# A planned kernel of four graph layers: LSTM gates by Tanh alone, the planner's order held on four engines, its margins drawn from a list

## The chip, the cores and the metric

The kernel runs on one core of one Trainium2 chip. The metric is the time of one execution on the device in microseconds (us); less is better. Times before and after are medians of several runs. A profile comes from one execution, taken by the hardware profiler.

In a core, TensorE (PE) multiplies matrices from SBUF into PSUM, and its weight loads (PEld) have a row of their own. VectorE (DVE), ScalarE (ACT) and GpSimd (POOL) work on elements, and SyncE (SP) issues DMAs. Each engine takes its instructions from a queue of its own, in a fixed order, and waits on semaphores for the others.

## What is computed

The input x has 128 graphs of 64 nodes with 256 features, in float32; all graphs share one 64x64 adjacency. Four layers follow, each closed by a residual sum and a LayerNorm:

```python
x = _layernorm(x + _L0_gnn_ref(x, adj, ...))   # normalised aggregation, two dense layers, two batch norms
x = _layernorm(x + _L1_gnn_ref(x, adj, ...))   # Laplacian (by its largest eigenvalue), attention, Gelu MLP
x = _layernorm(x + _L2_gnn_ref(x, adj, ...))   # two GCN layers, then LSTMs over windows of 1, 2, 3 and 4 nodes
x = _layernorm(x + _L3_gnn_ref(x, adj, ...))   # graph attention
```

The LSTM of layer 2 is the part whose formulas the change rewrites. Its last state overwrites the last node of each window, and the next window length reads what the one before wrote:

```python
g = x_t @ Wih.T + h @ Whh.T + bias
i, f, gg, o = jnp.split(g, 4, axis=-1)
c = sigmoid(f) * c + sigmoid(i) * tanh(gg)
h = sigmoid(o) * tanh(c)
```

## The kernel before, in words

The 8192 rows are cut into 16 blocks of 512 rows. A block is held in SBUF either with rows on the partitions (4 tiles of 128x256) or with features on the partitions (2 tiles of 128x512). Working memory is planned by hand: four PSUM tiles of 128x1024 (`PS`), and a stock of SBUF slots of the same size (`mem`) that grows as constants and earlier results fall out of use.

The order of the work is planned in Python while the program is written. Each task is a generator (`first_block`, `second_block`, `end_block`, `block`, `gcn_block`, `unit`, `last_block`, and a few for weights). At each `yield step(engine, us, ...)` (line 121) it says which engine its next instructions use, how long the planner should take them to last, how many PSUM tiles and slots they take, and from when they can run. `flow` (line 130) holds a clock for each engine. Again and again it picks one waiting step, advances the clock, and lets the generator write that step's instructions. Line 177 is the rule of choice: a step's time is the larger of its engine's free time and its own ready time plus the engine's margin. The earliest time wins, and ties go to the stream with the lower priority number. A margin so lets a step of a better stream pass another that would be ready a little earlier. Margins are 2.0 us for TensorE and 0.5 for VectorE and ScalarE (line 30). A step that names an activation table costs 1.3 us more when the table differs from the last one named (line 190).

There are two flows. The first (line 700) runs the eigenvalue loop and layer 0 up to its second batch norm. The second (line 1677) runs the rest in parallel streams: the blocks of layer 1 with the end of layer 0 (`seq`), the GCN with the one-step LSTM (`gcn`), the LSTM units of 2, 3 and 4 steps (`units`), and layer 3 (`last`, and `end` for the last four blocks in halves). The last three units have a stream of their own that needs no margin.

What the planner writes is not what the engines get. The framework's scheduler orders each engine's instructions again by its own estimate before it sets the waits.

The lines that the change touches:
- `stats` (line 264): bn_stats (L272) and bn_aggr (L273) for each of a block's four rows of tiles, then L274. Its users raise the result to the power -0.5 on POOL (L282, L294, L308).
- `ln_affine_steps` (line 289): LayerNorm with gain and bias on VectorE, two instructions per tile (L297, L300). `block` uses it twice.
- `ln_steps_act` (line 302): LayerNorm without them; VectorE makes -mean/std (L311), ScalarE applies it, one instruction per tile (L314).
- `lstm` (line 1036): one unit. The first step has no state: `products` (L1055), `gates` (L1067, bias inside), the product of i and tanh(g) on POOL (L1086), Tanh of the cell (L1094), the product with o on VectorE (L1102, or L1357 and L1389 where it is the last step). Later steps multiply by a Strassen scheme with seven products instead of eight (L1127), with sums on POOL (L1147, L1175) and VectorE (L1171, L1173, L1193, L1195), evictions on VectorE (L1186), gates on ScalarE (L1203, L1205, L1207), the product of i and tanh(g) on POOL (L1220), the cell on VectorE (L1228, L1231) and its Tanh (L1236).
- `plain_steps` (line 1251): later steps of the two half units at the end, without Strassen (L1264, L1266; gates L1269; the product on POOL L1280).
- Other long instructions on POOL: L634 in layer 0; L822, L860, L915, L916 and L933 in layer 1.
- Exp is at L854 and L1544, Gelu at L928. Evictions of PSUM that stand in the prediction: L749, L772, L898, L948, L1325 and L1345 on VectorE, L784 and L1353 on ScalarE.

Of the kernel before, what the change touches and what calls it, by code (L numbers as in the profile page):

```python
# [19 lines left out]
NT = 4  # L20
# [9 lines left out]
MARGIN = {"T": 2.0, "V": 0.5, "S": 0.5}  # L30
# [3 lines left out]
def kernel(ctx: ExitStack, tc: tile.TileContext, a: dict, out: bass.AP):  # L34
    nc = tc.nc
    V, S, G, T = nc.vector, nc.scalar, nc.gpsimd, nc.tensor

# [83 lines left out]
    def step(e, us, ps=0, sl=0, waits=True, at=None, tbl=None):  # L121

        return (e, us, ps, sl, waits, at, tbl)

    def flow(streams, margin):  # L130
# [6 lines left out]
        free = dict.fromkeys("TVSGQ", 0.0)  # L137
        table, running, now, seq = None, [], 0.0, 0
        while True:
# [31 lines left out]
            for r in running:  # L171
                e, us, ps, sl, _, at, tbl = r[2]
                at = at() if callable(at) else at
                if r[2][5] is not None and at is None:
                    continue
                t = r[3] if at is None else at
                soon = max(t if r[6].urgent else t + margin.get(e, 0.0), free[e])
                t = max(t, free[e])
                if (ps <= 0 or len(PS.free) >= ps) and (sl <= 0 or (len(mem.free) >= sl and safe(r, sl))):
                    if ps > 0:  # L180
                        t = max(t, PS.free[0][0])
                        soon = max(soon, PS.free[0][0])
                    if sl > 0:
                        t = max(t, heapq.nsmallest(sl, mem.free)[-1][0])
                        soon = max(soon, t)
                    if best is None or soon < least - 1e-9:
                        best, when, least = r, t, soon
            assert best is not None, "no task can go on"
            e, us, ps, sl, waits, at, tbl = best[2]
            if tbl is not None and tbl != table:  # L190
                us, table = us + 1.3, tbl
            end, now = when + us, when
# [84 lines left out]
    def ln_steps(y):  # L277

        yield step("V", 2.45)
# [3 lines left out]
        yield step("V", 1.9)  # L283
# [5 lines left out]
    def ln_affine_steps(y, g, b):  # L289

        yield step("V", 2.45)
        mv, rs = stats(y)
        yield step("G", 1.0)
        G.tensor_tensor(rs, rs, neghalf[:, :NT], ALU.pow)  # L294
        yield step("V", 3.4)
        for t in range(NT):
            V.scalar_tensor_tensor(y[:, t, :], y[:, t, :], mv[:, t, 0:1], g, ALU.subtract, ALU.mult)  # L297
            o = b if len(b.shape) == 2 else b[:, t, :]
            dst = y if len(b.shape) == 2 else b
            V.scalar_tensor_tensor(dst[:, t, :], y[:, t, :], rs[:, t : t + 1], o, ALU.mult, ALU.add)  # L300

    def ln_steps_act(y):

        n = y.shape[1]
        yield step("V", 0.6 * n)
# [6 lines left out]
        yield step("S", 0.6 * n)  # L312
# [93 lines left out]
    with c0:  # L406
# [129 lines left out]
        def bn_coeffs(name, nch, st, g, be):  # L536
# [4 lines left out]
            yield step("V", 0.3 * nch)  # L541
# [16 lines left out]
        def first_block(i):  # L558
# [6 lines left out]
            yield step("T", 1.15, ps=1, sl=1)  # L565
# [25 lines left out]
        def second_block(i):  # L591
# [27 lines left out]
            yield step("S", 2.8)  # L619
# [6 lines left out]
            yield step("V", 1.4, sl=2)  # L626
# [6 lines left out]
            yield step("G", 1.3, waits=False)  # L633
            G.tensor_tensor(T4, h[:, :, u], T2, ALU.subtract)  # L634
            yield step("V", 0.7)
# [98 lines left out]
    def end_block(i):  # L734
# [4 lines left out]
        yield step("S", 1.4)  # L739
# [15 lines left out]
    def block(i):  # L755
        x = X[i]
        mark("begun", i)
        yield step("T", 1.15, ps=1, sl=1)
# [15 lines left out]
        yield from ln_affine_steps(y, rows[:, names.index("g1"), :], rows[:, names.index("be1"), :])  # L774
        yield step("V", 1.25)
# [25 lines left out]
        yield step("T", 3.6, ps=1, sl=1)  # L801
# [19 lines left out]
        yield step("G", 2.4, waits=False)  # L821
# [3 lines left out]
        yield step("T", 1.15, ps=1, sl=1)  # L825
# [17 lines left out]
        yield step("V", 1.4, ps=-1)  # L843
# [5 lines left out]
        yield step("V", 2.5)  # L849
# [9 lines left out]
        yield step("G", 1.9)  # L859
# [13 lines left out]
        yield step("T", 1.15, ps=1, sl=1)  # L873
# [40 lines left out]
        yield step("G", 4.7, waits=False)  # L914
# [3 lines left out]
        for hf in range(2):  # L918
# [6 lines left out]
            yield step("S", 1.4, ps=-1, waits=hf == 1, tbl="gelu")  # L925
# [6 lines left out]
        yield step("G", 2.4, waits=False)  # L932
# [17 lines left out]
        yield from ln_affine_steps(y, rows[:, names.index("g3"), :], x)  # L950
# [25 lines left out]
    V.tensor_tensor(bl, bl, bh, ALU.add)  # L976

    def gcn_rows():
# [15 lines left out]
        PS.give(ps)  # L994
        mark("rows")
# [29 lines left out]
    def lstm(p, n, parts, x_of, out_of):  # L1025

        us = n * 1.68e-3
        v_us, g_us, s_us = (0.05 + n * r for r in (1.25e-3, 2.3e-3, 1.15e-3))  # L1030

        def bias(g, c):
            return bl[:, p - 1, 2 * g + c : 2 * g + c + 1]
# [30 lines left out]
        def gates(pair, t, ps, sl):  # L1064
            t = yield step("S", 0.1 + n * 2.5e-3, ps=-1, at=t, waits=False, tbl="sigmoid")
            for j, (g, c) in enumerate(pair):
                S.activation(of(sl)[:, j], fm(PS[ps])[:, j, :n], AF.Tanh if g == 2 else AF.Sigmoid, bias=bias(g, c))  # L1067
# [13 lines left out]
        for c in range(2):  # L1081
# [3 lines left out]
            t = yield step("G", g_us, at=t, waits=False)  # L1085
            G.tensor_tensor(of(s_cell)[:, c], of(sl)[:, 0], of(sl)[:, 1], ALU.mult)  # L1086
# [3 lines left out]
        for c in range(2):  # L1090
            sl = (sa, sb)[c]
            th = of(sl)[:, 1]
            t = yield step("S", s_us, at=tc_[c], waits=False, tbl="sigmoid")
            S.activation(th, of(s_cell)[:, c], AF.Tanh)  # L1094
            o = of(s_o)[:, c]
            t = yield step("V", v_us, at=max(t, t_o), sl=0 if p == 1 or c else 1, waits=False)
            if p == 1:
                last_h(c, o, th)
            else:
                if c == 0:  # L1100
                    s_h = mem.take()
                V.tensor_tensor(of(s_h)[:, c], o, th, ALU.mult)  # L1102
# [4 lines left out]
        if len(parts) == 1 and p > 1:  # L1107
            yield from plain_steps(p, n, us, of, bias, x_of, lambda ap: spread(ap, 0), last_h, s_cell, s_h, h_at)
# [27 lines left out]
        for s in range(1, p):  # L1136
# [3 lines left out]
            t_1 = yield step("G", g_us, sl=2, at=0.0, waits=False)  # L1140
# [28 lines left out]
            def differences():  # L1169
                yield step("V", two_us, at=h_at, waits=False)  # L1170
                V.tensor_tensor(T2, h_v, T1, ALU.subtract)  # L1171
                t_h.append((yield step("V", two_us, at=h_at, waits=False)))
                V.tensor_tensor(shaped(T3), shaped(h_v), x_v, ALU.subtract)  # L1173
                t_h.append((yield step("G", g_us, at=t_h[1], waits=False)))
# [22 lines left out]
            def stage4(g):  # L1197
                v, y = places(g)
                f = AF.Tanh if g == 2 else AF.Sigmoid
                t = yield step("T", us, at=max(t_h[2], at[g]), waits=False)  # L1200
                product(g, "A22", T4, v[:, 0, :])
                yield step("S", 0.1 + n * 1.15e-3, at=at[g, "0"], waits=False, tbl="sigmoid")
                S.activation(of(act[g])[:, 0], of(act[g])[:, 0], f, bias=bias(g, 0))  # L1203
                yield step("S", copy_us, at=at[g], waits=False, tbl="sigmoid")
                S.activation(y[:, 3, :], y[:, 3, :], f, bias=bias(g, 1))  # L1205
                at[g] = yield step("S", copy_us, ps=-1, at=t, waits=False, tbl="sigmoid")
                S.activation(y[:, 2, :], v[:, 0, :], f, bias=bias(g, 1))  # L1207
# [11 lines left out]
            t_g = yield step("G", 2 * g_us, at=at[2], waits=False)  # L1219
            G.tensor_tensor(of(act[2]), of(act[0]), of(act[2]), ALU.mult)  # L1220
# [6 lines left out]
            yield step("V", 2 * v_us, at=at[1], waits=False)  # L1227
            V.tensor_tensor(cell, cell, of(act[1]), ALU.mult)  # L1228
            mem.give(act[1])
            t = yield step("V", 2 * v_us, at=t_g, waits=False)  # L1230
            V.tensor_tensor(cell, cell, of(act[2]), ALU.add)  # L1231
# [3 lines left out]
            t = yield step("S", 2 * s_us, at=t, waits=False, tbl="sigmoid")  # L1235
            S.activation(of(act[2]), cell, AF.Tanh)  # L1236
            t = yield step("V", 2 * v_us, at=max(t, at[3]), sl=0 if last else 1, waits=False)
# [3 lines left out]
            else:  # L1241
                s_h = mem.take()
                V.tensor_tensor(of(s_h), of(act[3]), of(act[2]), ALU.mult)
# [6 lines left out]
    def plain_steps(p, n, us, of, bias, x_of, shaped, last_h, s_cell, s_h, h_at):  # L1250

        v_us, g_us, s_us = (0.05 + n * r for r in (1.25e-3, 2.3e-3, 1.15e-3))
        for s in range(1, p):
# [3 lines left out]
            def products(pair):  # L1257
# [9 lines left out]
                t = yield step("S", 0.3 + n * 2.1e-3, ps=-1, at=t, waits=False, tbl="sigmoid")  # L1267
                for j, (g, c) in enumerate(pair):
                    S.activation(of(sl)[:, j], fm(PS[ps])[:, j, :n], AF.Tanh if g == 2 else AF.Sigmoid, bias=bias(g, c))  # L1269
# [4 lines left out]
            for c in range(2):  # L1274
# [4 lines left out]
                tg = yield step("G", g_us, at=ta, waits=False)  # L1279
                G.tensor_tensor(A[:, 1], A[:, 0], A[:, 1], ALU.mult)  # L1280
                t = yield step("V", v_us, at=tb, waits=False)
                V.tensor_tensor(cell, cell, F[:, 0], ALU.mult)
                t = yield step("V", v_us, at=max(t, tg), waits=False)
                V.tensor_tensor(cell, cell, A[:, 1], ALU.add)
                t = yield step("S", s_us, at=t, waits=False, tbl="sigmoid")
                S.activation(A[:, 1], cell, AF.Tanh)
                ends.append((c, t, sa, sb))

            for c, t, sa, sb in ends:
                t = yield step("V", v_us, at=t, sl=0 if last or c else 1, waits=False)  # L1290
                if last:
                    last_h(c, of(sb)[:, 1], of(sa)[:, 1])
                else:
                    if c == 0:
                        h_new = mem.take()
                    V.tensor_tensor(of(h_new)[:, c], of(sb)[:, 1], of(sa)[:, 1], ALU.mult)
# [9 lines left out]
    def gcn_block(i):  # L1306
        yield step("T", 1.15, ps=1, sl=1)
# [21 lines left out]
        yield step("T", 1.15, ps=1, sl=1)  # L1329
# [12 lines left out]
        yield step("V", 1.4, ps=-1)  # L1342
# [13 lines left out]
        def out_of(q, c, o, th):  # L1356
            V.tensor_tensor(  # L1357
                hT_block(i)[:, c, :, :].rearrange("p n b -> p b n"), o, th, ALU.mult
# [9 lines left out]
    def unit(p, g, w0, nw, b0, nb):  # L1368
# [19 lines left out]
        def out_of(q, c, o, th):  # L1388
            V.tensor_tensor(half(src[:, c, :, p - 1, :], q), o, th, ALU.mult)  # L1389
# [22 lines left out]
    def sum_weights(p, sums):  # L1412
# [18 lines left out]
        for k in range(2):  # L1431
            i0, i1, h0, h1 = (w[:, k, :, c, :] for w in (ih, hh) for c in range(2))
            s1, s2, s3, s4 = (gates(sums[2 * i + k]) for i in range(4))
            for dst, y, z, op in (
# [5 lines left out]
                yield step("V", 0.7)  # L1440
# [15 lines left out]
    def last_block(i, t0=0, nt=NT):  # L1456
# [6 lines left out]
        yield step("S", 2.2 * r, sl=1)  # L1463
# [14 lines left out]
        V.tensor_tensor(x, px, x, ALU.add)  # L1478
# [260 lines left out]
```

## Time and profile before

| | |
|---|---|
| median of 3 runs (lowest, highest) | 2408.22 us (2407.28, 2410.26) |
| the profiled execution | 2409.44 us |
| its span, first to last instruction | 2407.7 us |
| mean granted TensorE clock | 0.982 of full speed |
| TensorE busy, idle in the span | 2287.2 us, 120.5 us |
| VectorE, ScalarE, POOL busy | 1287.7, 1187.4, 591.7 us |

The profile's busy time of an engine is the time in which one of its instructions runs. A group's row names line, engine, operation, output and inputs, shape and count; behind the bar are busy time, mean ns of one and the idle time just before them with what ended it. A timeline's row has start, duration, engine and line; in square brackets the idle time before it and the instruction that ended it. A row of the waits reads: who waited, for whom, us in total, times, longest. The granted clock is the share of TensorE's full speed that the hardware allowed. Times within the span are counted from its first instruction.

### The profile page before, as it was taken

To read this page: it belongs to the slowest core of one execution; us is meant where nothing else is said; L and a number is where in the kernel's file an instruction comes from. 1 tells how busy PE (TensorE), PEld (TensorE's weight loads), DVE (VectorE), ACT (ScalarE), POOL (GpSimd) and SP (SyncE) were. 2 spreads that over 40 slices of the span, in tenths; PEclk is the share of its full clock that TensorE was granted. 3 is DMA by queue.
4 is the path that set the end of the run, shared out by engine and by line. 5 is a ranking of instruction groups with operands and counts; after the bars stand their busy time and mean duration, and the time that the engine had idled before them with its cause. 6 is when DMAs were issued, how large, how long until landed. Compare 5 with 4: busy or idle time off the path is not lost.

```text
span 2407.7 us, 40603 instructions
## 1 busy us (share of the span) xinstructions
PE 2287.2 (95%) x16916; PEld 1759.9 (73%) x16916; DVE 1287.7 (53%) x2904; ACT 1187.4 (49%) x2189; POOL 591.7 (25%) x441
## 2 busy tenths in 40 slices
PE   8999788999989999999999999999999999998997
PEld 4548665666665666666667788899999888887785
DVE  4557678566483474744643433454444444455546
ACT  2257643544434544335453443444444653468766
POOL 0012134232242232331321222222221222122122
PEclk9999899999999999999999999999999999999998
DMA  6100301000000000001000000000001000001111
GB/s 162 49 1 1 111 23 49 28 10 10 1 12 17 10 10 10 1 10 36 36 19 27 18 1 1 17 2 1 1 1 36 1 10 9 19 27 66 40 36 45
DMA packets 42633, 57.91 MB, mean 24 GB/s; under 512 B 6224, under 2 KB 35536, under 8 KB 42448
## 3 DMA queue, kind: packets, MB, share of 16 engines
q1 hardware_dynamic: 41344, 54.22, 7.0%
q8 instruction: 133, 2.18, 0.4%
q10 hardware_dynamic: 1104, 1.08, 0.1%
q14 instruction: 52, 0.43, 0.1%
HBM read 38.52 MB, written 16.78 MB: 23 GB/s over the span
## 4 chain that ended last, share of the span: by engine, by line
PE 60%; DVE 16%; ACT 7%; POOL 3%; issue 2%; POOLq 0%; ACTq 0%; DVEq 0%
PE ps L1127 26%; PE ps L1055 11%; PE ps L365 7%; PE ps L377 4%; PE ps L938 4%; DVE ln_st L272 3%; ACT x L314 2%; PE ps L808 2%; POOL ln_rs L308 1%; PE ps L1507 1%; DVE x L300 1%; PE ps L341 1%; DVE ln_mv L273 1%; PE ps L353 1%; DVE ln_nm L311 1%
## 5 line engine op out<-in xcount | busy, mean ns | idle before, releaser
L1127 PE MATMUL ps<-x,x 128*128 128x256 f32 x928 | 225.0, 380 | 0.7 <-DVE t L1195 0.7
L1127 PEld LDWEIGHTS ps<-x,x 128*128 128x128 f32 x928 | 173.5, 190 | 24.9 <-issue 1.6
L314 ACT ACTIVATE x<-x,ln_nm,ln_rs 128x256 f32<-128x256 f32 x212 | 112.3, 592 | 133.3 <-DVE ln_nm L311 131.9
L1127 PE MATMUL ps<-t,x 128*128 128x256 f32 x672 | 163.7, 380 | 0.0
L1127 PEld LDWEIGHTS ps<-t,x 128*128 128x128 f32 x672 | 126.4, 190 | 17.1 <-DVE x L1195 0.8
L308 POOL TENSOR_TENSOR ln_rs<-ln_rs,neghalf 128x4 f32<-128x4 f32 (+1 forms) x72 | 71.2, 990 | 212.0 <-DVE ln_rs L274 186.4
L365 PE MATMUL ps<-t,W1T 128*128 128x512 f32 x256 | 117.8, 607 | 0.0
L1055 PE MATMUL ps<-h,wL 128*128 128x192 f32 (+2 forms) x480 | 103.9, 371 | 4.8 <-ACT h L1353 4.8
L272 DVE BATCH_NORM_STATS2 ln_st<-x 128x6 f32<-128x256 f32 x260 | 99.7, 403 | 0.4
L1055 PEld LDWEIGHTS ps<-h,wL 128*128 128x128 f32 x480 | 75.6, 192 | 29.9 <-issue 22.5
L294 POOL TENSOR_TENSOR ln_rs<-ln_rs,neghalf 128x4 f32<-128x4 f32 x32 | 36.9, 1153 | 217.1 <-DVE ln_rs L274 217.0
L1055 PE MATMUL ps<-h,x 128*128 128x256 f32 x384 | 86.7, 380 | 2.2 <-ACT t L1067 1.8
L1067 ACT ACTIVATE t<-ps,bih 128x512 f32<-128x512 f32 (+3 forms) x98 | 57.2, 634 | 55.8 <-PE ps L1055 55.1
L1203 ACT ACTIVATE x<-x,bih 128x512 f32<-128x512 f32 (+2 forms) x69 | 44.6, 648 | 80.3 <-DVE x L1193 80.0
L1186 DVE COPY x<-ps 128x256 f32<-128x256 f32 (+2 forms) x69 | 26.1, 378 | 108.4 <-PE ps L1127 107.6
L365 PEld LDWEIGHTS ps<-t,W1T 128*128 128x128 f32 x256 | 47.6, 195 | 49.6 <-issue 49.5
L365 PE MATMUL ps<-t,wA 128*128 128x512 f32 x160 | 76.8, 626 | 5.5 <-ACT t L784 5.5
L1055 PEld LDWEIGHTS ps<-h,x 128*128 128x128 f32 x384 | 72.6, 190 | 12.9 <-ACT t L1067 2.2
L1186 DVE COPY t<-ps 128x256 f32<-128x256 f32 (+2 forms) x51 | 18.8, 373 | 103.8 <-PE ps L1127 103.5
L1067 ACT ACTIVATE x<-ps,bih 128x512 f32<-128x512 f32 (+3 forms) x86 | 51.5, 650 | 40.6 <-PE ps L1055 40.4
L273 DVE BATCH_NORM_AGGREGATE ln_mv<-ln_st 128x2 f32<-128x6 f32 x448 | 71.3, 167 | 0.0
L1193 DVE TENSOR_TENSOR x<-ps,x 128x512 f32<-128x512 f32 (+2 forms) x69 | 41.4, 602 | 53.0 <-PE ps L1127 43.6
(714 smaller groups left out, 5713.2 us busy)
## 6 DMA issues: line engine op xcount, KB each, us to landing
t<-in_x_dram SPq DMA_DIRECT2D x26, 512.0 KB, 4.3
xd<-x SPq DMA_DIRECT2D x16, 512.0 KB, 2.6
x<-xd SPq DMA_DIRECT2D x8, 512.0 KB, 3.3
out_dram<-x SPq DMA_DIRECT2D x8, 512.0 KB, 2.9
h<-in_x_dram SPq DMA_DIRECT2D x5, 512.0 KB, 5.2
wL<-in_L_gnn_Wih_dram SPq DMA_DIRECT2D x2, 1024.0 KB, 5.0
x<-in_L_gnn_Whh_dram SPq DMA_DIRECT2D x2, 1024.0 KB, 5.4
x<-xd SPq DMA_DIRECT2D x5, 256.0 KB, 2.9
```

What stands on the lines that cost most here:

```text
L272: V.bn_stats(st[:, t, :], y[:, t, :])
L273: V.bn_aggr(mv[:, t, :], st[:, t, :])
L308: G.tensor_tensor(rs, rs, neghalf[:, :n], ALU.pow)
L314: S.activation(y[:, t, :], y[:, t, :], AF.Identity, scale=rs[:, t : t + 1], bias=nm[:, t : t + 1])
L365: T.matmul(ps[:, c, :], w[:, k, (off + c) * P : (off + c + 1) * P], yT[:, k, :], start=(k == 0), stop=(k == nk - 1),)
L377: T.matmul(ps[:, t, :], yT[:, k, t * P : (t + 1) * P], w[:, k, :], start=(k == 0), stop=(k == nk - 1),)
L808: T.matmul(pv[r * N : (r + 1) * N, b, :, :], x1T[:, k, b * N : (b + 1) * N], Wv_par[:, k, r, :, :], start=(k == 0), stop=(k == 1),)
L938: T.matmul(tm(PS[ps])[:, t, :], fm(mem[gs[k // 2]])[:, k % 2, t * P : (t + 1) * P], W2[:, k, :], start=(k == 0), stop=(k == 3),)
L1055: T.matmul(spread(fm(PS[ps])[:, j, :n], q), WL[p][0][:, k, m], x_of(0, q)[:, k], start=(k == 0), stop=(k == 1),)
L1067: S.activation(of(sl)[:, j], fm(PS[ps])[:, j, :n], AF.Tanh if g == 2 else AF.Sigmoid, bias=bias(g, c))
L1127: T.matmul(dst, WS[p][name](k, g), y[:, k], start=first and k == 0, stop=k == 1, skip_group_check=not first)
L1186: V.tensor_copy(y[:, 1, :], v[:, 0, :])
```

## The change

It has four parts.

**Gates by Tanh.** With sigmoid(z) = (1 + tanh(z/2))/2, each sigmoid becomes a Tanh of half the argument. The kernel keeps twice the cell and twice the state, and takes the halves back by scales and by instructions of the form (y + 1) * z on VectorE. The products that were on POOL (L1086, L1220, L1280) are such instructions now, so they move to VectorE.

**The LayerNorm with gain and bias** is gone as a step of its own. `block` calls `ln_steps_act` and then multiplies by the gain and adds the bias with two instructions over the whole block.

**The order.** The planner's order is held on TensorE, VectorE, ScalarE and POOL.

**The planner.** TensorE's margin goes from 2.0 to 0.5 us. Each margin is multiplied by a number from 0 to 2 that is drawn, for each task and each 50 us of planned time, from the list `DRAWS` (0 there means factor 1). Steps of VectorE and POOL that are marked "m" are planned so that one of VectorE does not begin while one of POOL runs. A change of the kind of matmul costs TensorE 0.1 us in the plan. Many planned costs are set anew. The second flow begins at the planned end of the first. The stream of the last three units is joined with the other units, and the stream `end` goes from priority 2 to 5.5.

The diff, cut to its core:

```diff
-MARGIN = {"T": 2.0, "V": 0.5, "S": 0.5}
+MARGIN = {"T": 0.5, "V": 0.5, "S": 0.5}
+STRETCH = 50.0
+DRAWS = [511, 307, 323, 0, 388, 0, 0, 35, 178, 58, 461, 150, 363, 205, 36, 263, 190, 963, 453, 309, 108, 239, 50, 391, 578, 171, 630, 639, 804, 485, 290, 771, 646, 0, 976, 942, 0, 370, 0, 0, 618, 674, 887, 378, 432, 790, 44, 487, 800, 1]
...
+    E = mybir.EngineType
+    ctx.enter_context(tc.manual_schedule(engines={E.PE, E.DVE, E.Activation, E.Pool}))
...
-    def flow(streams, margin):
+    def flow(streams, margin, start=0.0):
-        free = dict.fromkeys("TVSGQ", 0.0)
+        free = dict.fromkeys("TVSG", start) | {"Q": 0.0}
+        def drawn(k, t):
+            j = int(t / STRETCH)
+            d = DRAWS[j] if j < len(DRAWS) else 0
+            return (k * 7919 + j * 104729 + d * 1299709) * 2654435761 % 4294967296 / 2147483648 if d else 1.0
...
-                soon = max(t if r[6].urgent else t + margin.get(e, 0.0), free[e])
+                soon = max(t if r[6].urgent else t + margin.get(e, 0.0) * drawn(r[0][1], t), free[e])
                 t = max(t, free[e])
+                if e == "V" and tbl == "m":
+                    t, soon = max(t, locked), max(soon, locked)
...
-            if tbl is not None and tbl != table:
+            if e == "S" and tbl is not None and tbl != table:
                 us, table = us + 1.3, tbl
+            if e == "T" and tbl != shape:
+                us, shape = us + 0.1, tbl
+            if e == "G" and tbl == "m":
+                locked = when + us
...
-        yield from ln_affine_steps(y, rows[:, names.index("g1"), :], rows[:, names.index("be1"), :])
-        yield step("V", 1.25)
+        yield from ln_steps_act(y)
+        yield step("V", 3.7, tbl="m")
+        V.tensor_tensor(y, y, row["g1"], ALU.mult)
+        V.tensor_tensor(y, y, row["be1"], ALU.add)
         V.scalar_tensor_tensor(y, y, 0.0, x, ALU.max, ALU.add)
...
-        yield from ln_affine_steps(y, rows[:, names.index("g3"), :], x)
+        yield from ln_steps_act(y)
+        yield step("V", 2.45, tbl="m")
+        V.tensor_tensor(y, y, row["g3"], ALU.mult)
+        V.tensor_tensor(x, y, x, ALU.add)
...
-    V.tensor_tensor(bl, bl, bh, ALU.add)
...
+        V.tensor_tensor(bl, bl, bh, ALU.add)
+        for j in (slice(0, 4), slice(6, 8)):
+            V.tensor_scalar(bl[:, :, j], bl[:, :, j], 0.5, None, ALU.mult)
...
+        def gate(dst, z, g, c):
+            S.activation(
+                dst,
+                z,
+                AF.Tanh,
+                bias=bl[:, p - 1, 2 * g + c : 2 * g + c + 1],
+                scale=(1.0 if g == 2 else 0.5) * (1.0 if p == 1 else 0.5),
+            )
+
+        def times(dst, y, z):
+            V.scalar_tensor_tensor(dst, y, 1.0, z, ALU.add, ALU.mult)
...
-            t = yield step("G", g_us, at=t, waits=False)
-            G.tensor_tensor(of(s_cell)[:, c], of(sl)[:, 0], of(sl)[:, 1], ALU.mult)
+            t = yield step("V", v_us, at=t, waits=False, tbl="m")
+            times(of(s_cell)[:, c], of(sl)[:, 0], of(sl)[:, 1])
...
-            S.activation(th, of(s_cell)[:, c], AF.Tanh)
+            S.activation(th, of(s_cell)[:, c], AF.Tanh, scale=0.5)
...
-            t_g = yield step("G", 2 * g_us, at=at[2], waits=False)
-            G.tensor_tensor(of(act[2]), of(act[0]), of(act[2]), ALU.mult)
+            t_g = yield step("V", 2 * v_us, at=at[2], waits=False, tbl="m")
+            times(of(act[2]), of(act[0]), of(act[2]))
...
-            V.tensor_tensor(cell, cell, of(act[1]), ALU.mult)
+            times(cell, of(act[1]), cell)
...
-            V.tensor_tensor(cell, cell, of(act[2]), ALU.add)
+            V.scalar_tensor_tensor(cell, cell, 0.5, of(act[2]), ALU.mult, ALU.add)
...
-                tg = yield step("G", g_us, at=ta, waits=False)
-                G.tensor_tensor(A[:, 1], A[:, 0], A[:, 1], ALU.mult)
+                tg = yield step("V", v_us, at=ta, waits=False, tbl="m")
+                times(A[:, 1], A[:, 0], A[:, 1])
...
-        V.tensor_tensor(x, px, x, ALU.add)
+        V.scalar_tensor_tensor(x, px, 0.5, x, ALU.mult, ALU.add)
...
-            Stream(4, 2, end),
+            Stream(4, 5.5, end),
             Stream(2, 3, gcn),
             Stream(6, 4, seq),
-            Stream(2, 5, units[:-3]),
-            Stream(1, 1.5, units[-3:], urgent=True),
+            Stream(2, 5, units),
             Stream(4, 6, last),
         ],
         MARGIN,
+        start=done["bn2",],
     )
```

## The prediction, made before the changed kernel was run

> **What bounds the kernel now.** I read the page's busy shares first, then the busy times in four stretches that the slices suggest, then the list of waits of TensorE, then the timeline around its longest waits.
>
> ```profile
> span 2407.7 us, 40603 instructions
> PE 2287.2 (95%) x16916; PEld 1759.9 (73%) x16916; DVE 1287.7 (53%) x2904; ACT 1187.4 (49%) x2189; POOL 591.7 (25%) x441
> ```
>
> TensorE sets the time: 95% busy, no other engine near it. The change takes no matmul away, so it can only win TensorE's idle time and its slow time. Where those lie:
>
> ```profile
> 0.00:340.00 340.00, 300.64 (x2390) 200.09 (x2390) 203.67 (x437) 170.18 (x282) 48.60 (x51) 0.94 0.21 61
> 340.00:1320.00 980.00, 935.55 (x8541) 628.88 (x8534) 568.56 (x1216) 433.96 (x568) 299.63 (x183) 0.98 0.05 18
> 1320.00:2160.00 840.00, 835.62 (x4619) 756.09 (x4617) 384.38 (x773) 395.27 (x898) 193.80 (x142) 1.00 0.03 10
> 2160.00:2407.70 247.70, 215.35 (x1383) 174.86 (x1381) 131.14 (x481) 187.98 (x443) 49.71 (x65) 0.97 0.14 47
> ```
>
> Columns: length, then busy time of PE, PEld, DVE, ACT, POOL, then granted clock. TensorE idles 39.4, 44.4, 4.4 and 32.4 us: layer 0 with the filling of layer 1; layer 1 with the GCN and the one-step LSTMs; the longer LSTMs; the tail. The third stretch has nothing to win. A wait costs more than itself:
>
> ```profile
> 704.41 5.35 PE L365 MATMUL ps<-t,Wg 128*128 128x512 f32 x8 [1.96 <-DVE x L948]
> ...
> 714.22 3.70 PE L365 MATMUL ps<-t,wA 128*128 128x512 f32 x8
> ```
>
> The same eight matmuls take 1.65 us longer after a wait of 1.96 us: the clock record shows half speed for 3.4 us from 704.4. From 340 to 1320 seven such stretches hold 27.4 us of busy time, 13.7 us lost; in the tail 10.1 and 5.1; before 340, 30.6 and 15.3. The Trainium skill (TensorE: Matmul & The Clock Gate, Part 1) has the clock drop after an idle window of about 3.4 us. Here 1.96 us sufficed. By its rule shorter waits would cost only themselves; by the row they cost about 1.7 us more.
>
> **What the waits are made of.** Around 977 to 991:
>
> ```profile
> 977.21 2.35 POOL L916 TENSOR_TENSOR x<-x,rows 128x1024 f32<-128x1024 f32 x1
> 977.27 3.36 DVE L300 SCALAR_TENSOR_TENSOR t<-t,ln_rs,rows 128x256 f32<-128x256 f32 x3 [0.51 <-POOL ln_rs L294]
> ...
> 984.56 2.36 POOL L933 TENSOR_TENSOR x<-x,rows 128x1024 f32<-128x1024 f32 x1 [5.00 <-DVE t L776]
> 985.54 2.46 DVE L852 TENSOR_TENSOR h<-h,mx 128x1024 f32<-128x1024 f32 x1
> ...
> 990.69 4.11 PE L365 MATMUL ps<-x,wB 128*128 128x512 f32 x5 [3.86 <-DVE h L1325]
> ```
>
> VectorE's L300 (0.48 us each by median, 1.28 for three undisturbed) and L852 (1.22) end when POOL's long instruction ends. VectorE is late by 3.3 us, the eviction at L1325 stands behind it, TensorE waits 3.86 us. The same pattern stands before three of the other five longest waits between 340 and 1320: L274 took 2.14 us instead of 0.17 at 370.0 (wait 5.53), L311 2.29 instead of 0.16 at 406.6 (4.67), and four L300 took 5.85 at 710.1, where three take 1.28 undisturbed (4.26). Instructions with an operand in PSUM (L1193 takes 0.69 either way) and the bn_stats (0.40) do not stretch. Over the whole run I sum about 119 us of such stretching, each overlapped instruction against the median of its form.
>
> **The change, part by part.**
>
> Tanh alone. The trace has 79 table loads of 1.28 us, 101 us of ACT:
>
> ```profile
> L928 ACT ACT_TABLE_LOAD x18 | 23.1, 1283 | 3.2 <-issue 2.3 <-PE ps L365 0.6
> L1067 ACT ACT_TABLE_LOAD x17 | 21.8, 1283 | 33.9 <-PE ps L1055 33.7
> L1544 ACT ACT_TABLE_LOAD x16 | 20.5, 1283 | 5.5 <-DVE mx L1540 5.3
> ```
>
> With the Sigmoids dropped from ACT's order as traced, Gelu and Exp alternate 23 times, 22 of them before 1400. So 56 loads go, 72 us of ACT, 26 loads (33 us) of them in the tail. At 2221.0 a Tanh (L1094) follows an Exp load with no load between, so Exp and Tanh share a table. The Trainium skill (ScalarE: Activation LUTs, What ACT_TABLE_LOAD costs) gives 2.66 us for a switch with its drain; by that 56 loads would be 149 us. No such drain is to be seen: at 722.15 a load takes 1.28 and the Gelu begins at 723.44.
>
> POOL to VectorE. The products L1086 (74), L1220 (33) and L1280 (12) take 162.7 us on POOL. On VectorE they cost some 86: 128x512 at 0.69 (L1102), 128x1024 at 1.22 (L776), narrower ones by the rows between, 128x256 at 0.42. POOL falls to 429, and over a third of its long instructions, the ones that stretch VectorE's, are gone.
>
> The affine normalisation. Per use, eight L297 and L300 of 0.48 leave VectorE; two products of 1.22 and one L311 of 0.16 come; ACT gets four L314, 2.07 us together. For 32 uses: VectorE 40 us less before any stretching, ACT 66 more. The sums: ACT 1187 - 72 + 66 = 1181, DVE about 1288 - 40 + 86 = 1334 less what stretching goes. Neither comes near TensorE. Latency of one use grows by about 1 us (0.16 + 2.07 + 2.44 - 3.84); other blocks cover it, except while layer 1 fills.
>
> Scaling by 0.5, the halved biases and the (y+1)z form cost nothing beyond the same instructions: L776, of that form, takes 1.22 for 1024 columns as the plain L772 does. The halved biases add two or three short VectorE instructions inside the GCN's preparation.
>
> Order, costs and margins. TensorE now keeps the planner's order; so do VectorE, ACT and POOL. The trace shows that before they did not: a bn_stats of the next row (L272 x2) runs ahead of the bn_aggr (L273) written before it. What the order is worth is not in the trace; none of the waits, or all, are its bounds, and losses are the last rival. The planner now holds VectorE's two-operand steps back while POOL runs, which is what the four waits above lacked.
>
> **The sum**, against the profiled execution's 2409.4 us:
> - 340 to 1320: 44.4 + 13.7 = 58.1 at stake. The six longest waits are 23.6 us; four, 18.3 of it, have a stretch of VectorE ahead, 11 us in all. That pays for about half; tables, shorter VectorE work and the order should give some more. I take two thirds: 39 (bounds 0 and 58).
> - Tail: ACT ended 13.4 us of waits; with the 5.1 us of slow clock 18.5. Its loads there were 33 us of 188. Two thirds: 12 (bounds 0 and 28, the waits before the last matmul with the clock).
> - Before 340: until 260 the waits are the start (7.0 and 4.0) and the batch norm's barrier (5.8), which no order takes away. From there 20.0 idle and 10.4 of slow clock, but one block's latency rules while the pipe fills, and that grows by 1 us a use. I take 4 (bounds -4 and 20).
> - 1320 to 2160: 0.
>
> Together 55: 2354 us. The median of the runs is 1.2 us below the profiled execution; I keep 2354 for both.
>
> **The rivals.**
>
> *Nearly all of it comes back*: 58 + 28 = 86, 2323 us. For it: all three causes are attacked at once. Against it: the steps L274 and L311, which stretched too, are not marked in the planner. 11%.
>
> *Loads stay*: if Gelu's table lacks Tanh, every Gelu and Tanh keep alternating; 48 loads, 62 us, stay on ACT from 340 to 1320. ACT ended 18.3 us of the waits there; two thirds of these stay: 2366. The trace has no Tanh right after a Gelu. The Trainium skill (ScalarE: Activation LUTs, Table sets) lists Tanh with Exp's and Sigmoid's sets and not with Gelu's. 4%.
>
> *Given back*: the held order brings as many waits as go from 340 to 1320, and the tail alone wins: 12 to 20 us, 2393. 10%; that nothing measurable is left, 5%.
>
> *Slower*: the product L1220 goes onto VectorE's queue in the third stretch, where TensorE has no slack.
>
> ```profile
> POOL x L1220 <- ACT x L1207: 97.0, 13, 19.5
> POOL t L1220 <- ACT t L1207: 66.8, 7, 23.9
> ```
>
> POOL sat through 164 us for these gates. If VectorE stands there instead, the evictions L1186, L1193 and L1195 behind it are late, and TensorE needs their results a product later. Two us at each of 33 steps are 66: 2354 + 66 = 2420. It decides from 1.7 us a step (55/33). For it: a queue held in a model's order cannot step past a late gate. Against it: VectorE is 46% busy there, and the plan places the product by the gate's end. 18%.
>
> **How the numbers follow.** Forecast (2330 to 2380) 52%, loads stay 4%, nearly all 11%, given back 10%: faster 77%. Within 0.2%, about what a measurement of this kernel can tell from no change, 5%. Slower 18%. The range runs from 2316, below the second case, to 2413, leaving out the slower case and a little below.
>
> **What would show it.** Right: no Sigmoid, some 23 loads, none in the tail; POOL near 430 us; idle of TensorE from 340 to 1320 under 25 us and at most four half-speed stretches there; the third stretch still over 99% busy. Wrong: waits of TensorE on L1186 or L1193 spread over the third stretch, VectorE stretched as often as before, or over 45 loads.

## The result, and the profile after

The changed kernel takes 2354.93 us (median of 4 runs, 2354.07 to 2356.48), the kernel before 2407.75 (4 runs). The ratio is 0.9779, with a 95% interval of 0.9762 to 0.9796. The profiled execution took 2355.12 us. Of the five executions of e6_sigmoid below, one took 10391 us at a granted clock of 0.215: its median of 2399.62 us counts that one (2399.27 without it), and its profile is of another.

```profile
span 2353.0 us, 40443 instructions
PE 2266.4 (96%) x16916; PEld 1753.1 (75%) x16916; DVE 1365.9 (58%) x2865; ACT 1167.2 (50%) x2257; POOL 435.4 (19%) x322
```

(In the kernel before, `stats`, `lstm` and `plain_steps` begin at lines 265, 1025 and 1250.) The span is 54.7 us shorter. TensorE does the same 16916 matmuls; its idle time fell from 120.5 to 86.6 us, its busy time by 20.8. The four stretches of the span, with the columns as before:

```profile
0.00:340.00 340.00, 300.52 (x2463) 202.05 (x2464) 204.33 (x427) 166.73 (x280) 42.55 (x49) 0.94 0.21 61
340.00:1320.00 980.00, 972.79 (x8696) 664.50 (x8695) 620.05 (x1145) 486.42 (x716) 267.62 (x152) 1.00 0.05 19
1320.00:2160.00 840.00, 820.85 (x4697) 745.61 (x4696) 418.31 (x893) 393.39 (x946) 94.64 (x81) 1.00 0.03 11
2160.00:2353.00 193.00, 172.25 (x1064) 140.93 (x1063) 123.16 (x402) 120.62 (x317) 30.57 (x40) 0.95 0.14 49
```

TensorE's idle time is now 39.5, 7.2, 19.1 and 20.8 us. Nearly the whole gain stands in the second row: 37.2 us of idle gone, and a clock of 1.00 instead of 0.98. Not one half-speed stretch is left there, where seven had cost 13.7 us. The five longest waits of TensorE in it (before, six of them summed to 23.6 us):

```profile
PE ps L364 <- ACT h L746: 1.6, 2, 1.2
PE ps L346 <- issue: 1.3, 1, 1.3
PE ps L382 <- ACT h L898: 1.2, 1, 1.2
PE ps L358 <- ACT h L768: 1.1, 1, 1.1
PE ps L1153 <- DVE t L1350: 0.5, 1, 0.5
```

In each row the last number is the longest wait: none is over 1.3 us. The stretches are cut by time, and by 1320 TensorE has done 53 us more work than before (busy time, with half speed counted as half), so what followed came earlier. The tail idles 20.8 us in place of 32.4, but the stretch before it 19.1 in place of 4.4. From 1320 to the end TensorE idles 39.9 us in place of 36.7, and its half-speed busy time there is 8.8 us in place of 10.1: the two together gave nothing. The longest group of waits in the third stretch, and one of layer 3 in it:

```profile
PE ps L1153 <- DVE t L1221: 3.7, 4, 1.8
PE ps L364 <- ACT h L1580: 1.5, 1, 1.5
```

The table loads, which were 79:

```profile
L935 ACT ACT_TABLE_LOAD x9 | 11.5, 1283 | 8.0 <-PE ps L370 7.8
L861 ACT ACT_TABLE_LOAD x8 | 10.3, 1283 | 0.5 <-DVE h L859 0.4
L589 ACT ACT_TABLE_LOAD x1 | 1.3, 1283 | 11.6 <-DVE t L577 11.6
L1569 ACT ACT_TABLE_LOAD x1 | 1.3, 1283 | 0.0
```

L935 is Gelu, L861 and L1569 are Exp, L589 is the first load of the run. No load stands before an LSTM gate (L1049), and 420 of that line's 666 instructions run with Gelu's load as the last one before them, so Gelu's table holds Tanh.

### The profile page after: what moved, and what is told of

Read it like the earlier page. It is cut to its first block, busy times and chain, and to the rows that moved or that the text cites. A ratio compares the mean times of both kernels' runs of the same rounds, so it can differ in the third digit from the quotient of the medians.

```text
span 2353.0 us, 40443 instructions
## 1 busy us (share of the span) xinstructions
PE 2266.4 (96%) x16916; PEld 1753.1 (75%) x16916; DVE 1365.9 (58%) x2865; ACT 1167.2 (50%) x2257; POOL 435.4 (19%) x322
## 4 chain that ended last, share of the span: by engine, by line
PE 80%; issue 8%; DVE 7%; ACT 4%; POOL 0%; DMA 0%; ACTq 0%; POOLq 0%; DVEq 0%
PE ps L1153 27%; PE ps L1081 14%; PE ps L370 11%; PE ps L382 6%; PE ps L945 4%; PE ps L645 3%; PE ps L346 2%; PE ps L815 2%; PE ps L1532 2%; PE ps L1289 2%; PE ps L1291 2%; PE ps L358 2%; DVE ln_st L290 1%; PE ps L364 1%; DVE ln_mv L291 1%
## 5 line engine op out<-in xcount | busy, mean ns | idle before, releaser
L1153 PE MATMUL ps<-t,x 128*128 128x256 f32 x928 | 226.8, 380 | 0.3 <-DVE x L1221 0.3
L1153 PEld LDWEIGHTS ps<-t,x 128*128 128x128 f32 x928 | 173.0, 190 | 22.8 <-issue 1.6
L1049 ACT ACTIVATE t<-ps,bih 128x512 f32<-128x512 f32 (+5 forms) x185 | 98.2, 568 | 159.7 <-PE ps L1081 103.7
L1153 PE MATMUL ps<-x,x 128*128 128x256 f32 x608 | 147.5, 380 | 1.5 <-DVE t L1221 1.1
L1049 ACT ACTIVATE x<-ps,bih 128x512 f32<-128x512 f32 (+5 forms) x159 | 82.2, 548 | 106.3 <-PE ps L1081 67.9
L1153 PEld LDWEIGHTS ps<-x,x 128*128 128x128 f32 x608 | 114.4, 190 | 17.2 <-DVE t L1221 1.8
L290 DVE BATCH_NORM_STATS2 ln_st<-x 128x6 f32<-128x256 f32 x244 | 97.6, 400 | 0.7
L1049 ACT ACTIVATE x<-x,bih 128x512 f32<-128x512 f32 (+5 forms) x134 | 69.3, 564 | 51.8 <-DVE x L1219 49.7
L1081 PE MATMUL ps<-t,wL 128*128 128x512 f32 x216 | 94.6, 594 | 0.2 <-ACT t L1378 0.2
L1081 PEld LDWEIGHTS ps<-h,wL 128*128 128x128 f32 x456 | 69.6, 190 | 17.8 <-issue 16.0
L1212 DVE COPY x<-ps 128x256 f32<-128x256 f32 (+2 forms) x67 | 25.5, 381 | 98.4 <-PE ps L1153 98.4
L316 DVE SCALAR_TENSOR_TENSOR ln_nm<-ln_mv,ln_rs 128x4 f32<-128x4 f32 (+1 forms) x104 | 61.4, 593 | 33.2 <-POOL ln_rs L313 33.1
L319 ACT ACTIVATE t<-t,ln_nm,ln_rs 128x256 f32<-128x256 f32 x112 | 58.5, 591 | 41.0 <-DVE ln_nm L316 40.9
```

The lines of the kernel that those rows point to most:

```text
L290: V.bn_stats(st[:, t, :], y[:, t, :])
L316: V.scalar_tensor_tensor(nm, mv[:, :, 0], -1.0, rs, ALU.mult, ALU.mult)
L319: S.activation(y[:, t, :], y[:, t, :], AF.Identity, scale=rs[:, t : t + 1], bias=nm[:, t : t + 1])
L1049: S.activation(dst, z, AF.Tanh, bias=bl[:, p - 1, 2 * g + c : 2 * g + c + 1], scale=(1.0 if g == 2 else 0.5) * (1.0 if p == 1 else 0.5),)
L1081: T.matmul(spread(fm(PS[ps])[:, j, :n], q), WL[p][0][:, k, m], x_of(0, q)[:, k], start=(k == 0), stop=(k == 1),)
L1153: T.matmul(dst, WS[p][name](k, g), y[:, k], start=first and k == 0, stop=k == 1, skip_group_check=not first)
```

## The experiments

Two theories went in. A: the gain is the planned order, with costs that fit, and holds only if it reaches the engines. B: the gain is less work on ScalarE and POOL, and any sensible order earns it. The kernel before took 2407.35 to 2407.79 us beside these runs. Seven of the kernels were run only twice (e11_hold_pe, e4_before_tanh, e2_nodraws, e12_best30, e8_worst, e5_nolock, e7_affine), and the two times lie up to 5.9 us apart, so differences of a few us between these kernels are not settled. "Stretched" below is the time by which VectorE's instructions that overlap a POOL instruction of over 1.2 us exceed the median of their form elsewhere, summed over the run. "Idle" is TensorE's from 340 to 1320. Each of these edits also gives the engines another order, since the planner or the framework's scheduler then chooses anew.

| kernel | median us | idle | stretched |
|---|---|---|---|
| before | 2407.75 | 44.4 | 119 |
| changed | 2354.93 | 7.2 | 99 |
| e1_free: changed, order not held | 2421.86 | 56.4 | 85 |
| e11_hold_pe: changed, held on TensorE alone | 2447.05 | 60.9 | 87 |
| e3_before_held: before, its own plan held | 2425.65 | 26.7 | 118 |
| e4_before_tanh: before, with the new LSTM | 2382.28 | 24.7 | 93 |
| e2_nodraws: changed, empty list | 2372.72 | 10.2 | 93 |
| e12_best30: changed, another list | 2372.80 | 7.5 | 87 |
| e8_worst: changed, a bad list | 2431.11 | 39.8 | 79 |
| e5_nolock: empty list, marks not used | 2385.55 | 15.9 | 95 |
| e6_sigmoid: empty list, LSTM of before | 2399.62 | 15.1 | 104 |
| e7_affine: empty list, LayerNorm of before | 2385.89 | 22.5 | 90 |
| e9_marked: two more marks, own list | 2351.83 | 11.0 | 65 |
| e10_nopool: and four POOL instructions on VectorE | 2348.95 | 7.3 | 14 |

### The held order

```diff
-    ctx.enter_context(tc.manual_schedule(engines={E.PE, E.DVE, E.Activation, E.Pool}))
```

> The changed kernel with one edit: the order is not held, so the framework orders each engine's instructions again. Theory A, the searched order is the gain and holds only if it reaches the engines: 30 to 45 us of the 53 are lost, 2385 to 2400. Theory B, the gain is less work on ScalarE and POOL (56 table loads, the products, the stretching) and any sensible order earns it: 2350 to 2362.

2421.86 us, ratio to before 1.0057 (1.0034 to 1.0080): not only is the gain gone, the kernel is slower than before. B falls for the change as a whole. It has the same 19 table loads as the changed kernel, the same products on VectorE and less stretching. From 340 to 1320 TensorE's idle time is 49.2 us more than in the changed kernel, and half speed costs 23.0 us where it cost nothing. What the framework's order does can be read from its timeline around the longest wait of the second stretch (its lines are those of the changed kernel less 2):

```profile
842.95 3.70 PE L368 MATMUL ps<-t,Wg 128*128 128x512 f32 x8 [1.16 <-ACT t L1358]
...
845.23 2.35 POOL L938 TENSOR_TENSOR x<-x,rows 128x1024 f32<-128x1024 f32 x1 [5.54 <-DVE t L781]
...
846.13 1.47 DVE L290 TENSOR_SCALAR ln_rs<-ln_mv 128x4 f32<-128x4 f32 x1
...
849.05 1.58 ACT L317 ACTIVATE x<-x,ln_nm,ln_rs 128x256 f32<-128x256 f32 x3 [5.25 <-DVE ln_nm L314]
...
850.54 1.00 ACT L799 ACTIVATE t<-ps 128x1024 f32<-128x1024 f32 x1
851.45 0.59 ACT L317 ACTIVATE x<-x,ln_nm,ln_rs 128x256 f32<-128x256 f32 x1
852.07 1.23 DVE L779 TENSOR_TENSOR x<-x,rows 128x1024 f32<-128x1024 f32 x1 [3.11 <-ACT x L317]
853.33 1.22 DVE L780 TENSOR_TENSOR x<-x,rows 128x1024 f32<-128x1024 f32 x1
854.47 1.28 DVE L1368 TENSOR_TENSOR t<-ps,rb 128x512 f32<-128x512 f32 x2
...
855.84 1.06 ACT L1376 ACTIVATE t<-t 128x1024 f32<-128x1024 f32 x1 [3.81 <-DVE t L1368]
...
856.95 2.93 PE L1079 MATMUL ps<-t,wL 128*128 128x512 f32 x3 [5.76 <-ACT t L1376]
```

The eviction L1368 has its matmuls done at 846.65. It stands in VectorE's queue behind L779 and L780 of another block. L779 waits 3.11 us for the last L317, and ScalarE has put an eviction (L799) between the third L317 and the fourth. VectorE idles with the eviction ready behind it, and TensorE waits 5.76 us. No table load is in this. One step on the way is stretched (L290, 1.47 us), but the step of POOL that uses its result stands in POOL's queue behind L938 and could not have begun before 847.58 either way. The wait comes of queues that cannot be passed.

```diff
-    ctx.enter_context(tc.manual_schedule(engines={E.PE, E.DVE, E.Activation, E.Pool}))
+    ctx.enter_context(tc.manual_schedule(engines={E.PE}))
```

> The changed kernel with the order held on TensorE alone; the framework orders VectorE, ScalarE and POOL again. If the 67 us that the run without any held order lost come from the queues of VectorE and ScalarE: 2405 to 2430. If TensorE's own order is what counts: 2355 to 2370.

2447.05 us, past what either theory gave. Holding TensorE's order alone is 25 us worse than holding none: its longest waits from 340 to 1320 are for ScalarE's evictions (12.2 us in three waits for one group). So TensorE's own order is not enough. The waits fit a loss in the queues of the element engines that a held TensorE makes larger; no run holds VectorE, ScalarE or POOL without the others, so which of them matters is not shown.

```diff
+    E = mybir.EngineType
+    ctx.enter_context(tc.manual_schedule(engines={E.PE, E.DVE, E.Activation, E.Pool}))
```

> The kernel before with its own plan held on the four engines, and nothing else. If holding alone pays, because the framework's second ordering spoils the plan: 2385 to 2400. If the plan before, with its margin of 2 us for TensorE and its costs, was no better than the framework's order: 2405 to 2430. Theory B: 2400 to 2415.

2425.65 us, ratio 1.0075 (1.0052 to 1.0098): the second of the three. Holding does not pay by itself. Its four-stretch view shows the exchange:

```profile
340.00:1320.00 980.00, 953.28 (x8612) 648.82 (x8605) 610.86 (x1229) 451.93 (x598) 306.06 (x186) 0.98 0.05 18
1320.00:2160.00 840.00, 810.12 (x4428) 729.01 (x4427) 369.93 (x728) 375.72 (x872) 186.54 (x138) 1.00 0.03 8
```

Layer 1 gains 17.7 us of idle, and the LSTM stretch loses 25.5 (29.9 in place of 4.4), in many short waits on its gates and additions:

```profile
PE ps L1129 <- ACT x L1209: 5.8, 8, 1.3
PE ps L1129 <- ACT t L1209: 4.5, 7, 1.3
PE ps L1129 <- DVE t L1197: 3.5, 5, 1.8
```

This is the prediction's slower rival in its form, many waits of about a microsecond under a held order, though not through L1220, which is still on POOL here.

### Tanh alone

```diff
-                S.activation(of(sl)[:, j], fm(PS[ps])[:, j, :n], AF.Tanh if g == 2 else AF.Sigmoid, bias=bias(g, c))
+                gate(of(sl)[:, j], fm(PS[ps])[:, j, :n], g, c)
...
-            t = yield step("G", g_us, at=t, waits=False)
-            G.tensor_tensor(of(s_cell)[:, c], of(sl)[:, 0], of(sl)[:, 1], ALU.mult)
+            t = yield step("V", v_us, at=t, waits=False)
+            times(of(s_cell)[:, c], of(sl)[:, 0], of(sl)[:, 1])
```

> The kernel before with the LSTM's gates by Tanh and its products on VectorE, with its old planner, old LayerNorm and the framework's order. Theory B: 25 to 40 us faster, 2370 to 2383, most of it in the tail, where 33 us of table loads go. Theory A: 2395 to 2410.

2382.28 us (two runs, 2379.35 and 2385.21), ratio 0.9893 (0.9863 to 0.9922): as B had it in size, but not in place. Idle from 340 to 1320 fell from 44.4 to 24.7 us, where the loads fell too. After 1320 it rose from 36.7 to 37.8, though the loads there went. The other way round, inside the new plan:

```diff
+                S.activation(of(sl)[:, j], fm(PS[ps])[:, j, :n], AF.Tanh if g == 2 else AF.Sigmoid, bias=bias(g, c))
...
+            t = yield step("G", g_us, at=t, waits=False, tbl="m")
+            G.tensor_tensor(of(s_cell)[:, c], of(sl)[:, 0], of(sl)[:, 1], ALU.mult)
```

> As the run with the empty list (2372.7 us), but with the LSTM of before: Sigmoid and Tanh gates, their table loads, and the products on POOL (marked, with the costs of before, so that the planner knows them). If Tanh alone is worth the same inside the new plan as in the old one (25 us there): 2393 to 2403. If the held plan hides the loads: within 8 us of 2372.7.

2399.62 us, 27 more than with the empty list alone, with 60 loads. The new LSTM is worth 25 us without the held order and 27 with it. Both runs change the gates and move the products at once; no run separates the table loads from the products.

### The list and the planner's marks

```diff
-DRAWS = [511, 307, 323, 0, 388, 0, 0, 35, ...
+DRAWS = []
```

> The changed kernel with an empty list DRAWS, so each margin is its plain 0.5 us; all else as changed, order held. Theory A: the list is worth some 20 to 30 us, 2375 to 2385, with waits of TensorE back between 340 and 1320. Theory B: 2353 to 2362.

2372.72 us: the list is worth 17.8 us, outside both ranges and a little under the 20 expected by A. The waits did not come back between 340 and 1320 (10.2 us of idle). Idle rose by 4.7 us from 1320 to 2160 and by 5.7 after it. The span is 16.4 longer, and the rest is spread.

```diff
+DRAWS = [138, 583, 868, 822, 783, 65, 262, 121, ...
```

> The changed kernel with another list DRAWS: the one that the planner itself finds the latest end for among thirty random lists. If the planner's end tells the chip's time, as a search in its model needs: 2415 to 2435, 60 us or more behind the changed kernel. If the lists differ in the model only: 2360 to 2380, near the empty list.

2431.11 us, as A had it: 76 us behind the changed kernel with the same instructions. Here the waits are back from 340 to 1320, 39.8 us; two of them, of 15.2 and 14.8 us, are most of it. It also has less stretching (79 us) than the changed kernel (99).

```diff
+DRAWS = [299, 241, 889, 967, 619, 799, 978, 733, ...
```

> The changed kernel with the list that the planner finds best among thirty random ones; its planned end is 2 us behind that of the empty list. If the planner's end tells the chip's time to within a few us: 2370 to 2380, by the empty list's 2372.7. If lists of one planned end differ much on the chip: more than 10 us away from 2372.7, and then differences of that size between the single edits above say nothing.

2372.80 us, 0.1 from the empty list, where the two runs of each lie 2.0 and 2.3 us apart. Two orders that the planner puts 2 us apart are equal on the chip here within that, which is what a search in its own model needs. It is one pair.

```diff
-                if e == "V" and tbl == "m":
-                    t, soon = max(t, locked), max(soon, locked)
```

> As the run with the empty list (2372.7 us), and the planner no longer keeps VectorE's marked steps apart from POOL's: the marks are ignored where a step is placed. If the planner's knowledge of the stretching is a main cause (the prediction's reading of the four waits): 2385 to 2400, the stretched time of VectorE up from 93 us to 115 or more, waits back between 340 and 1320. If it is the held order with fitting costs and not the marks: within 8 us of 2372.7.

2385.55 us, 12.8 behind the empty list, just inside the first range. From 340 to 1320 idle is 5.8 us more and half speed costs 5.1 us in place of nothing, so waits are back there. But the stretched time hardly moved (95 and 93; from 340 to 1320, 82 and 76), far from the 115 expected. So the marks keep little from being stretched; at most they let the plan fit better. That a single other order would differ by 13 us for no cause is unlikely by the run before, but it was tried once.

```diff
-        yield from ln_steps_act(y)
-        yield step("V", 3.7, tbl="m")
-        V.tensor_tensor(y, y, row["g1"], ALU.mult)
-        V.tensor_tensor(y, y, row["be1"], ALU.add)
+        yield from ln_affine_steps(y, rows[:, names.index("g1"), :], rows[:, names.index("be1"), :])
+        yield step("V", 1.25)
```

> As the run with the empty list (2372.7 us), but with the LayerNorm with gain and bias of before, on VectorE alone. If the shorter work of VectorE matters: 2380 to 2390. If it is neither gain nor loss, as TensorE has no wait left between 340 and 1320: within 6 us of 2372.7. A little faster before 340, where the new form is about 1 us longer per use.

2385.89 us, 13.2 behind the empty list, in the first range. Idle from 340 to 1320 is 22.5 us instead of 10.2: as far as this one order shows, the work that VectorE is spared pays here. No gain shows before 340 (39.3 us idle and 38.9).

### The stretching

In the changed kernel the short step L316 had grown the most:

```profile
L316 DVE SCALAR_TENSOR_TENSOR ln_nm<-ln_mv,ln_rs 128x4 f32<-128x4 f32 (+1 forms) x104 | 61.4, 593 | 33.2 <-POOL ln_rs L313 33.1
```

```diff
-        yield step("V", 0.2)
+        yield step("V", 0.2, tbl="m")
...
+        yield step("V", 0.15, tbl="m")
+        floor(mv, rs)
```

> The changed kernel, with the two short steps of a LayerNorm on VectorE that the planner had left unmarked (L292 as a step of its own, and L316) marked too, and a new list DRAWS found for this planner. If the planner's error is these two (L316 takes 0.59 us a piece where 0.16 is its undisturbed time, 43 us over the run): 2343 to 2351, faster than the changed kernel, and the time of L316 down by half. If stretching is harmless where the held order has put it: 2352 to 2362, no gain.

2351.83 us, ratio 0.9766 (0.9749 to 0.9782), which overlaps the changed kernel's interval. The row of that run has a mean of 410 ns in place of 593, a fall of a third and not of half. The time lies between the two ranges. A gain of 3 us is likely but not settled.

```diff
-        yield step("G", 4.7, waits=False, tbl="m")
-        G.tensor_tensor(y, y, row["g2"], ALU.mult)
-        G.tensor_tensor(y, y, row["b2"], ALU.add)
+        yield step("V", 2.45, waits=False, tbl="m")
+        V.tensor_tensor(y, y, row["g2"], ALU.mult)
+        V.tensor_tensor(y, y, row["b2"], ALU.add)
```

> As the run before, and the four long instructions of a layer 1 block on POOL (L828, L922, L923, L940 of the changed kernel) are on VectorE, with a list of its own. It takes away what stretches VectorE between 340 and 1320 and adds some 78 us of work to VectorE. If stretching costs TensorE time there: 2340 to 2350. If it does not, and VectorE's queue gets longer for nothing: 2358 to 2370.

2348.95 us (2347.18 to 2353.09, 4 runs), ratio 0.9758 (0.9744 to 0.9773): the fastest of all, each run below the lowest of the changed kernel (2354.07). The short step in its profile:

```profile
L323 DVE SCALAR_TENSOR_TENSOR ln_nm<-ln_mv,ln_rs 128x4 f32<-128x4 f32 (+1 forms) x104 | 18.9, 185 | 37.4 <-POOL ln_rs L320 37.4
```

The stretching is gone (185 ns each; 14 us in the run), and VectorE's busy time fell to 1346.7 us although it took on four more long instructions a block. Yet all that is worth 6 us against the changed kernel, and not from 340 to 1320, where idle is 7.3 us as it was (7.2). It is 12.2 us from 1320 to 2160 instead of 19.1, and 25.3 after that instead of 20.8, in the profiled execution of 2353.09 us. The list differs and VectorE has the added work, so the 6 us are of all three. Against the run before it is 2.9 us, with times that overlap, and idle from 340 to 1320 of 7.3 us for 11.0.

## Why the prediction came out right, point by point

The time (2354.93 for 2354) is nearer than its parts, and that is luck. The sum took 11.9 us too little from 340 to 1320 and 2.0 too little in the tail, 16.4 too much from 1320 to 2160 and 1.5 too much before 340. Another 3.9 us came from TensorE's own work, for which it had no term.

- **What bounds**: right. TensorE's work at full speed (busy time less half of what runs at half speed) is 2253.2 us before and 2249.3 after. The change won idle time and slow clock. The 3.9 us between these were not traced.
- **340 to 1320, taken at 39**: 37.2 of idle and 13.7 of clock, 50.9. The step that was mis-sized is the share of two thirds; 88% of the 58.1 came back.
- **Tail, taken at 12**: from 2160 on idle fell by 11.6 us and the half-speed loss by 2.4, 14.0 together. ScalarE ended 5.4 us of the waits there instead of 13.4, and the loads went (31 after 1400 before, one now). As the prediction cut the span, the term held in size. Its cause did not show: in e4_before_tanh, under the old planner and without the loads, idle from 2160 is 28.1 us and half speed costs 10.1 in place of 5.1, so the loads alone won nothing there.
- **Before 340, taken at 4**: idle the same (39.4 and 39.5), 2.6 of clock.
- **1320 to 2160, taken at 0 and over 99% busy**: this step failed. It is 97.7% busy, with 14.7 us more of idle and 1.7 of half speed, 16.4 lost. The sum took the work of each stretch as fixed, but the order moved it: 364 matmuls of layer 3's own lines (from L1481 on) lie in this stretch now, 176 before. Of the waits there 9.7 us have such a line on one side (0.7 before) and 9.2 have none (3.2 before), the longest group 3.7 us on L1221. So what the tail won was lost here: from 1320 to the end ScalarE ended 16.7 us of waits, and 15.9 before.
- **Tables**: 23 expected, 19 found. POOL 435.4 for 429. ScalarE 1167 for 1181. VectorE 1365.9 for at most 1334: the sum expected stretching to fall, and the short step L316 alone takes 61.4 us where 104 undisturbed ones would take 17.
- **The cause of the waits**: half wrong. The four waits did have a stretched instruction ahead, but the stretched time fell by a sixth only (119 to 99; from 340 to 1320, 88 to 83) while the waits there fell by five sixths. "VectorE stretched as often as before" was to be a sign of being wrong, and there it nearly is. The kernel with the worst list has less of it than the changed one, and taking nearly all of it away from the changed kernel wins 6 us. What made them waits was an eviction behind it in a fixed queue, and the order settles that. How much of the four waits a kernel before without stretching would keep was not tried.
- **The order**: the prediction could bound it only by none and all. It is worth 67 us within the changed kernel, with this one list, more than the whole change; held on the plan before, it costs 18.
- **Loads stay**: fell. The rival's 2366 counted 18.3 us of waits ended by ScalarE from 340 to 1320 where the trace has 20.1, and one of its 48 loads stands at 12.2 us; with 20.1 it would have been 2367. The Trainium skill (ScalarE: Activation LUTs, Table sets) names Tanh with Exp's and Sigmoid's sets; 19 loads, none of them before a gate, show that Gelu's has it here too.
- **The clock**: as the row had it. Between 1829.5 and 1832.5 two waits of 1.82 and 0.47 us were followed by 3.4 us of half speed, again below the idle window of the Trainium skill (TensorE: Matmul & The Clock Gate, Part 1). Not every such wait is: in the kernel before, waits of 1.88 us at 1144.5 and 1.84 at 1287.7 had no half speed after them, one of 1.39 at 1030.7 had, and in e8_worst one of 3.23 at 1898.7 had none. So the 1.7 us that the prediction adds to a short wait are what it can cost, not what it always costs.
- **Slower, by L1220 on VectorE**: it did not decide. VectorE does stand for such gates:

```profile
DVE x L1059 <- ACT x L1049: 55.3, 21, 6.9
DVE t L1059 <- ACT t L1049: 43.0, 17, 8.2
```

These are products that moved there from POOL, with others of their form. TensorE's waits on the evictions behind them from 1320 to 2160 stay at 0.5 us (L1212) and 4.4 us (L1221), so little that is urgent stands behind a late gate in this plan. The run with no held order shows, for a LayerNorm, what it looks like when something does.

The parts do not add up one by one: the new LSTM is worth 25 to 27 us, the list 18, the LayerNorm 13 with an order not fitted to it, the held order 67 in the new plan and -18 in the old. The 13 us of the LayerNorm, like the 13 of the marks, are no larger than what another list alone can do (18), and their planned ends are not known.

## What to carry to other kernels

A held order is worth what the plan behind it is worth: holding it won with the new plan and lost with the old. Holding TensorE alone was worse here than holding all four or none; other choices were not run. Whether the plan's costs rank orders as the chip does can be tested with two orders of nearly one planned end and one order that the plan finds bad. When an engine waits, ask what stands ahead of the late instruction in its queue; a slow instruction is only late if something urgent is behind it. Removing all of a visible nuisance (85 us of stretched instructions) can be worth 6 us, and a number that comes out right can hide wrong terms, so compare stretch by stretch, and ask whether the same work still lies in each.

## What the runs showed that was not expected

- With the same instructions in other orders the kernel takes 2354.93 to 2447.05 us, a spread of 3.9%.
- TensorE's order held alone costs 25 us more than no held order at all (2447.05 and 2421.86).
- A short instruction of 128x4 on VectorE (L316) takes 0.16 us undisturbed and 2.3 us (the median of the 27 that overlap a POOL instruction of over 1.2 us), about as long as POOL's long instructions themselves (L940 takes 2.4).
- The clock gains with the waits: with no wait over 1.3 us from 340 to 1320 there is not one half-speed stretch there, where seven stood before.
